# Attention scores from high and low halves of queries and keys in three single passes

## The chip, the cores and the metric

The kernel runs on one core of a Trainium2 chip. The metric is the device time of one execution, in microseconds. A core has TensorE for matrix products (PE, with its weight loads shown apart as PEld), VectorE (DVE), ScalarE (ACT), GpSimd (POOL) and SyncE (SP), which here only issues transfers. TensorE writes to PSUM, eight banks of 128 partitions by 512 float32.

## The reference

Two layers of cross attention are applied to `x` of shape (32, 256, 320). Each has 20 heads of 16 channels, and a context of 77 rows of 512 channels per batch. The context has exactly 77 rows, so only the text part of each layer has keys; the slices for objects, others and images are empty.

```python
q = split_heads(x @ Wq); k = split_heads(ctx @ Wk); v = split_heads(ctx @ Wv)
p = softmax(q @ k.T / sqrt(16))          # over the 77 keys
x = merge_heads(p @ v) @ Wo + bo + x     # layer 0, then layer 1 with its own weights
```

All of it is float32.

## The kernel before

Everything lies with channels on the partitions. Two batches make a pair, and one pair in one layer is a unit `u`; there are 32 units, taken in an order in which layer 0 runs four pairs ahead of layer 1. A unit's 320 channels by two batches are held as five groups `g` of 128 channels by 256 positions (`NG = 5`, `of_group`); the fifth group holds the last 64 channels of both batches. A group has eight heads. Four row blocks `j` of 32 channels hold two heads each, which the code counts by `e`.

Per unit, in the order of the data:

- `queries` or `outputs_and_queries` project the queries `q`; `keys` and `keys_rest` project the keys `kR` (two groups, two groups, one group). ACT copies them out of PSUM. `mask_keys` makes `kT`: for each `e` the keys with the other head's channels set to zero, on POOL (for unit 0 on DVE).
- `maxima` multiplies queries by `kT` for some halves `h` of a group (128 positions each, ten halves in a unit) into four banks `psm`, one for each `j`, and DVE reduces each bank to the largest score of every position and head. `turn` transposes those maxima on DVE into `mT` and writes them by small transfers into rows of the queries: one spare channel of the other head carries the maximum.
- `less_keys` makes `kM` on POOL: the masked keys with -1 in that spare channel, so that `scores` gets score less maximum from one product. As the spare channel belongs to the other head, the queries exist twice (`q[0]`, `q[1]`, the second a copy by a transfer).
- `scores(u, g)` makes the eight products of a group into four banks `pss`; ACT takes the exponential into `pT`. `products` multiplies by the values into one bank `po`, with a column of ones for the sums; `divide` transposes it on DVE (`turned`), takes the reciprocal (`inv`) and multiplies on POOL (`normal`); `turn_back` transposes on DVE into `oT`. `outputs_and_queries` projects the outputs of one unit (`psy`) and the queries of another. `vals` projects the values of a chunk of context rows (`psv`), and `place_vals` puts them in place by transfers.

All PSUM tiles come from one pool of eight banks handed out in turn (`bank`). The order of the instructions is written by hand: each step is put at a slot and a place in the slot (`at`), and each engine carries out its own instructions strictly in that order. `start(u)` is the first slot of unit `u`; four units take 17 slots. Within a slot the places follow one another in this order:

```python
    order = (
        "load", "maxima", "turn back", "turn", "scores", "values", "rest", "back", "full", "last",
    )
```

With `s = start(u - 2)`, a unit's keys stand at `s - 2`, `s - 1` and `s + 1` ("rest"; the last is `keys_rest`), its queries at `s`, its maxima from `s + 1` on, up to three halves a slot and none in a slot with two score groups, and its scores from `start(u)`. Units with `u % 4 > 0` have their first two score groups in one slot. The products of a group stand one slot after its scores.

Of the kernel before, what the change touches and what calls it, by code (L numbers as in the profile page):

```python
# [51 lines left out]

F32 = mybir.dt.float32
AF = mybir.ActivationFunctionType
ALU = mybir.AluOpType
AX = mybir.AxisListType
# [3 lines left out]
P = 128  # L60
# [34 lines left out]
def xattn_kernel(ctx: ExitStack, tc: tile.TileContext, xT, cT, cP, weights, outT):  # L95
# [14 lines left out]
    xs, cs, cvs = {}, {}, {}  # L110

    def load_x(p):
        x_sb = io.tile([P, NX], F32, tag="x", name=f"x_{p}", bufs=AHEAD + 3)
        xs[p] = x_sb
        if p == 0:
            for a, b in ((0, NT), (NT, 2 * NT), (2 * NT, NX)):
                nc.sync.dma_start(out=x_sb[:, a:b], in_=xT[p, :, a:b])
        else:
            (nc.scalar if p == 1 else nc.sync).dma_start(out=x_sb, in_=xT[p])
# [34 lines left out]
    make_identity(nc, ident)  # L154


    stages, maxes = [[], []], []
    for layer in range(2):
        for i in range(2):

            v = const.tile([P, HEADS // 2, 2, 2, HD], F32, name=f"stage_{layer}_{i}")
            nc.gpsimd.memset(v, 1.0)
            stages[layer].append(v)
    for i in range(2):
        m = const.tile([P, 2 * NG, 32], F32, name=f"max_{i}")
        nc.gpsimd.memset(m, 0.0)
        maxes.append(m)

    ctx.enter_context(tc.manual_schedule())

# [4 lines left out]
    nc.vector.tensor_reduce(masks, r32.rearrange("p (e d) -> p e d", d=HD), AX.X, ALU.add)  # L175

    less = const.tile([P, 2], F32, name="less")
    for e in range(2):
        i = HD * (1 - e)
        nc.vector.tensor_scalar_mul(less[:, e : e + 1], r32[:, i : i + 1], -1.0)  # L180


    warm = bank("warm")
# [80 lines left out]
        for e in range(2):  # L264
            engine.tensor_scalar_mul(kT[:, e], kR[:, groups], masks[:, e : e + 1])  # L265

    def less_keys(u):

        kR = st[u].pop("kr")
        kM = st[u]["km"] = work.tile([P, 2, NG, L], F32, tag="kM", name=f"kM_{u}", bufs=3)  # L270
        for e in range(2):
            nc.gpsimd.tensor_scalar(
                kM[:, e], kR, masks[:, e : e + 1], less[:, e : e + 1], ALU.mult, ALU.add
            )

    def keys(u, t):
        p, layer = units[u]
# [32 lines left out]
        mask_keys(u, 2)  # L310

    def new_queries(u):
        st[u]["q"] = [
            work.tile([P, NX], F32, tag=f"q{e}", name=f"q{e}_{u}", bufs=3) for e in range(2)
        ]
        return st[u]["q"][0]

    def queries(u):

        p, layer = units[u]  # L320
        w = w_sb[layer]
        q0 = new_queries(u)
        ps = [[bank(f"psq_{u}_{t}_{b}") for b in range(NB)] for t in range(2)]
        if u == 0:

            main_channels(ps, w["q"], xs[p], start=True, stop=False)
            last_channels(ps, w["q2"], xs[p], start=False, stop=True)
        else:
# [9 lines left out]
        if u > 0:  # L338
            nc.sync.dma_start(out=st[u]["q"][1], in_=q0)

    def queries_rest(u):

        p, layer = units[u]
        w = w_sb[layer]
        q0, q1 = st[u]["q"]
# [3 lines left out]
        nc.sync.dma_start(out=q1, in_=q0)  # L349

    def outputs_and_queries(u, uq):

        w, wq, o, x = w_sb[units[u][1]], w_sb[units[uq][1]], st[u]["o"], xs[units[uq][0]]
        q0 = new_queries(uq)
        y = [[bank(f"psy_{u}_{t}_{b}") for b in range(NB)] for t in range(2)]
        main_channels(y, w["o"], o, start=True, stop=False)
        y2 = bank(f"psy_{u}_2")
        rest_main(y2, w["o"], o, start=True, stop=False)


        q2 = bank(f"psq_{uq}_2")
# [24 lines left out]

    def load_chunk(layer, i):
        n = min(P, B * L - i * P)
# [41 lines left out]
    def place_vals(u, i):  # L430

        p, layer = units[u]
        if "v" not in st[u]:
            st[u]["v"] = work.tile(
                [P, NB, HEADS // 2, 2, 2, HD], F32, tag="v", name=f"v_{u}", bufs=3
            )
        for b in range(NB):
            first = (p * NB + b) * L
# [16 lines left out]
    def maxima(*parts):  # L455
# [1 line left out]
        ps = [bank(f"psm_{parts[0][0]}_{parts[0][1]}_{j}") for j in range(4)]  # L457
        steps = [(u, h) for u, first, n in parts for h in range(first, first + n)]
        for i, (u, h) in enumerate(steps):
            g, c = h // 2, h % 2  # L460
            q, kT = of_group(st[u]["q"][0], g), st[u]["k", g // 2]
            for j in range(4):
                r = slice(32 * j, 32 * j + 32)
                nc.tensor.matmul(  # L464
# [6 lines left out]
        for j in range(4):  # L471
            at = 0
            for u, first, n in parts:
                nc.vector.tensor_reduce(  # L474
                    maxes[u % 2][:, first : first + n, 2 * j : 2 * j + 2],
                    ps[j][:, at * 2 * L : (at + n) * 2 * L].rearrange(
                        "p (c e k) -> p c e k", e=2, k=L
                    ),
# [3 lines left out]
                at += n  # L482

    def turn(u):
        mT = work.tile([P, 2 * NG * 32], F32, tag="mT", name=f"mT_{u}", bufs=2)
        nc.vector.transpose(mT, maxes[u % 2].rearrange("p k i -> p (k i)"))
        for e in range(2):
            q = st[u]["q"][e].rearrange("(j i) n -> i j n", i=32)[HD * (1 - e)]
            for a in range(P // 32):
                queue = nc.scalar if u == 0 and a == 3 else nc.sync  # L490
                queue.dma_start(
                    out=q.rearrange("j (k a n) -> a j k n", a=P // 32, n=32)[a],
                    in_=mT[32 * a + e : 32 * a + 8 : 2].rearrange("j (k n) -> j k n", n=32),
                )


    def scores(u, g):
        kM = st[u]["km"]
        ps = [bank(f"pss_{u}_{g}_{j}") for j in range(4)]
        for e in range(2):  # L500
            q = of_group(st[u]["q"][e], g)
            for j in range(4):
                r = slice(32 * j, 32 * j + 32)
                nc.tensor.matmul(  # L504
                    ps[j][:L, e * S : (e + 1) * S], kM[r, e, g, :], q[r, :],
                    start=True, stop=True,
                )
        st[u]["p", g] = [probs.tile([P, 512], F32, tag="pT", name=f"pT_{u}_{g}_{j}") for j in range(4)]
        for j in range(4):
            nc.scalar.activation(st[u]["p", g][j][:L], ps[j][:L], AF.Exp, scale=SCALE)  # L510

    def products(u, g):
        vpad = st[u]["v"]
        if "o" not in st[u]:
            st[u]["o"] = work.tile([P, NX], F32, tag="oT", name=f"oT_{u}", bufs=3)
        po = bank(f"po_{u}_{g}")
        pT = st[u].pop(("p", g))
        for e in range(2):
# [106 lines left out]
    for u, (p, layer) in enumerate(units):  # L625
# [82 lines left out]
    at(-6, "rest", lambda: less_keys(0))  # L708
# [4 lines left out]
    at(-1, "rest", lambda: less_keys(1))  # L713
# [5 lines left out]
    for u, slot in ((1, 1), (2, 4)):  # L719
# [34 lines left out]
def pack(wq, wk, wv, wo, bias):  # L754

    out = np.zeros((P, WIDE), np.float32)

    def put(name, rows):
        at, n, width = PARTS[name]
# [72 lines left out]
```

## Time and profile before

| | |
|---|---|
| time, median of 3 runs | 949.21 us (948.82 to 950.74) |
| span of the profiled execution | 947.2 us |
| median of the runs less that span | 2.0 us |
| granted TensorE clock in the profiled execution | 1.000 |
| chain that ended last | PE 99% |
| its largest lines | po 16.6%, psy 15.3%, pss 15.1%, psq 14.8%, psm 11.3%, psv 8.8%, psk 7.2% |
| DMA, mean over the span | 88 GB/s, 83.78 MB |
| q copied to q by transfer | 32 issues of 640 KB |
| maxima into the queries | 254 issues of 5 KB on SP |

The page was taken on one execution; the profile gives no time for that execution other than its span, and the times are those of runs without a profile. A busy share is that of the whole span. A wait is put down to what ended last; the idle time before a group of instructions is that of the engine just before them. Matmuls are pipelined, so the busy time of a group is not the time that it takes from the others: that is read from the distance of starts.

### The profile page before, as it was taken

To read this page: it belongs to the slowest core of one execution; us is meant where nothing else is said; L and a number is where in the kernel's file an instruction comes from. 1 tells how busy PE (TensorE), PEld (TensorE's weight loads), DVE (VectorE), ACT (ScalarE), POOL (GpSimd) and SP (SyncE) were. 2 spreads that over 40 slices of the span, in tenths; PEclk is the share of its full clock that TensorE was granted. 3 is DMA by queue.
4 is the path that set the end of the run, shared out by engine and by line. 5 is a ranking of instruction groups with operands and counts; after the bars stand their busy time and mean duration, and the time that the engine had idled before them with its cause. 6 is when DMAs were issued, how large, how long until landed. Compare 5 with 4: busy or idle time off the path is not lost.

```text
span 947.2 us, 46546 instructions
## 1 busy us (share of the span) xinstructions
PE 940.9 (99%) x20942; PEld 630.3 (67%) x20942; DVE 533.2 (56%) x1195; ACT 431.8 (46%) x975; POOL 254.0 (27%) x422
## 2 busy tenths in 40 slices
PE   9999999999999999999999999999999999999998
PEld 7666766666666676667766666666667666666654
DVE  3465545655555555555656565655555655665564
ACT  2355343553435544355434455335454454544562
POOL 2233212332123321223322233212332223332211
PEclk9999999999999999999999999999999999999999
DMA  6553112232132321323222222322222221222102
GB/s 228 191 160 111 60 58 61 87 127 62 72 105 68 112 71 69 108 72 99 74 74 94 71 96 74 116 67 90 72 85 90 89 89 37 75 93 63 51 33 85
DMA packets 54825, 83.78 MB, mean 88 GB/s; under 512 B 15780, under 2 KB 36580, under 8 KB 54626
## 3 DMA queue, kind: packets, MB, share of 16 engines
q1 hardware_dynamic: 53674, 78.29, 25.4%
q8 instruction: 165, 2.70, 1.2%
q10 hardware_dynamic: 952, 2.50, 0.7%
q14 instruction: 34, 0.28, 0.1%
HBM read 35.39 MB, written 10.49 MB: 48 GB/s over the span
## 4 chain that ended last, share of the span: by engine, by line
PE 99%; DVE 0%; issue 0%
PE po L524 17%; PE psy L194 15%; PE pss L504 15%; PE psq L194 15%; PE psm L464 11%; PE psv L194 9%; PE psk L194 7%; PE psy L228 4%; PE psq L228 4%; PE psk L302 2%; PE warm L185 0%; PE psv L418 0%; DVE max L474 0%; DVE x L566 0%; DVE ones L152 0%
## 5 line engine op out<-in xcount | busy, mean ns | idle before, releaser
L510 ACT ACTIVATE pT<-pss 77x512 f32<-77x512 f32 x640 | 324.4, 593 | 191.3 <-PE pss L504 190.4
L474 DVE TENSOR_REDUCE max<-psm 128x6 f32<-128x462 f32 (+2 forms) x512 | 248.5, 550 | 242.7 <-PE psm L464 242.7
L545 POOL TENSOR_TENSOR normal<-turned,inv 128x256 f32<-128x256 f32 x160 | 99.1, 620 | 655.6 <-DVE inv L540 655.6
L524 PE MATMUL po<-pT,v 77*32 77x256 f32 x2560 | 165.9, 384 | 0.1
L194 PE MATMUL psy<-oT,w 128*32 128x256 f32 (+1 forms) x3072 | 164.4, 380 | 0.0
L504 PE MATMUL pss<-q,kM 32*77 32x256 f32 x2560 | 163.9, 376 | 0.0
L194 PE MATMUL psq<-x,w 128*32 128x256 f32 (+1 forms) x3072 | 151.5, 379 | 0.0
L194 PEld LDWEIGHTS psy<-oT,w 128*32 128x32 f32 (+1 forms) x3072 | 88.2, 108 | 63.6 <-issue 14.8
L536 DVE STREAM_TRANSPOSE turned<-po 128x512 f32<-128x512 f32 x160 | 109.2, 682 | 34.8 <-PE po L524 34.8
L524 PEld LDWEIGHTS po<-pT,v 77*32 77x32 f32 x2560 | 72.3, 109 | 80.2 <-DVE max L474 34.0
L194 PEld LDWEIGHTS psq<-x,w 128*32 128x32 f32 (+1 forms) x3072 | 86.1, 109 | 53.1 <-ACT pT L510 0.9
L265 POOL TENSOR_SCALAR kT<-kR,masks 128x154 f32<-128x154 f32 x186 | 111.7, 612 | 20.2 <-ACT kR L291 20.2
L504 PEld LDWEIGHTS pss<-q,kM 32*77 32x77 f32 x2560 | 98.8, 141 | 26.8 <-DVE oT L559 4.0
L464 PE MATMUL psm<-kT,q 32*128 32x154 f32 x2560 | 115.4, 306 | 0.0
L464 PEld LDWEIGHTS psm<-kT,q 32*128 32x128 f32 x2560 | 89.7, 183 | 32.7 <-issue 24.8
L566 DVE SCALAR_TENSOR_TENSOR x<-psy,w,x 128x256 f32<-128x256 f32 x160 | 69.2, 478 | 73.2 <-PE psy L194 72.0
L194 PE MATMUL psv<-w,cv 128*32 128x160 f32 x2432 | 93.6, 299 | 0.3 <-DVE max L474 0.3
L559 DVE STREAM_TRANSPOSE oT<-normal 128x256 f32<-128x256 f32 x160 | 67.4, 433 | 43.1 <-POOL normal L545 43.1
L381 ACT COPY q<-psq 128x256 f32<-128x256 f32 x28 | 10.4, 372 | 162.0 <-PE psq L228 162.0
L194 PEld LDWEIGHTS psv<-w,cv 128*32 128x32 f32 x2432 | 77.9, 110 | 4.3 <-DVE max L474 0.7
L194 PE MATMUL psk<-c,w 128*32 128x154 f32 x2048 | 78.8, 294 | 0.0
L194 PEld LDWEIGHTS psk<-c,w 128*32 128x32 f32 x2048 | 66.2, 110 | 11.9 <-DVE max L474 0.6
(35 smaller groups left out, 449.0 us busy)
## 6 DMA issues: line engine op xcount, KB each, us to landing
q<-q SPq DMA_DIRECT2D x32, 640.0 KB
c<-in_cP_dram SPq DMA_DIRECT2D x32, 308.0 KB
cv<-in_cT_dram SPq DMA_DIRECT2D x38, 256.0 KB
out_dram<-x SPq DMA_DIRECT2D x15, 640.0 KB
x<-in_xT_dram SPq DMA_DIRECT2D x14, 640.0 KB
v<-stage SPq DMA_DIRECT2D x26, 192.5 KB
q<-mT SPq DMA_DIRECT2D x254, 5.0 KB
w<-in_w_dram ACTq DMA_DIRECT2D x2, 640.0 KB
```

The source lines that it names most:

```text
L194: nc.tensor.matmul(out[m : m + 32], lhsT[:, m : m + 32], rhs, **flags)
L228: nc.tensor.matmul(ps[o : o + 32, 0:S], lhsT, rhs, **flags)
L265: engine.tensor_scalar_mul(kT[:, e], kR[:, groups], masks[:, e : e + 1])
L464: nc.tensor.matmul(ps[j][:, i * 2 * L : (i + 1) * 2 * L], q[r, c * P : (c + 1) * P], kT[r, :, g % 2, :], start=True, stop=True,)
L474: nc.vector.tensor_reduce(maxes[u % 2][:, first : first + n, 2 * j : 2 * j + 2], ps[j][:, at * 2 * L : (at + n) * 2 * L].rearrange("p (c e ...
L504: nc.tensor.matmul(ps[j][:L, e * S : (e + 1) * S], kM[r, e, g, :], q[r, :], start=True, stop=True,)
L510: nc.scalar.activation(st[u]["p", g][j][:L], ps[j][:L], AF.Exp, scale=SCALE)
L524: nc.tensor.matmul(po[o : o + 32, e * S : (e + 1) * S], vpad[:L, b, pair, e].rearrange("p a d -> p (a d)"), pT[j][:L, e * S : (e + 1) * S] ...
L536: nc.vector.transpose(turned[:, 0 : 2 * S], po)
L545: nc.gpsimd.tensor_tensor(normal.rearrange("p q e d -> p e q d"), outs, inv.unsqueeze(3).broadcast_to([P, 2, S // 32, HD]), ALU.mult,)
L559: nc.vector.transpose(of_group(st[u]["o"], g), normal)
L566: nc.vector.scalar_tensor_tensor(x, ps[:, 0:S], w_sb[layer]["b"][:, 0, t : t + 1], x, ALU.add, ALU.add)
```

## The change

The kernel no longer puts the maximum in a spare channel and no longer multiplies in float32 for the scores. Queries and keys are split into a high half, rounded by writing it as `float32r`, and a low half, the exact rest. The score product then has 16 channels times two query halves on its 32 rows; the keys stand there twice, and one matmul with the keys' high half and one with their low half add up. Ahead of them, one matmul of 512 columns with a constant of -1 (`less`) and the split maxima as rows (`max_rows`) writes the maximum into each bank. All are `float32r`. The maxima themselves stay float32 products.

The halves are made by POOL (for unit 0 by DVE), `split_keys` and `split_queries` in three pieces, and put in place by SP's transfers, `spread_keys` (four a unit) and `spread_queries` (twelve a unit). `turn` splits the maxima on DVE before the transpose and issues four transfers. The heads of a pair are interleaved by channel (`pack` reorders the columns of the weights on the host), so the masks change. In `maxima` the half `h` now is group `h % 5`, position block `h // 5`. `v`, `oT` and the new tiles have two buffers, `x` six instead of seven; the values are made one unit later.

```diff
     def load_x(p):
-        x_sb = io.tile([P, NX], F32, tag="x", name=f"x_{p}", bufs=AHEAD + 3)
+        x_sb = io.tile([P, NX], F32, tag="x", name=f"x_{p}", bufs=AHEAD + 2)
...
+    maxes = const.tile([P, 2, 4, 32], F32, name="maxes")
...
+        m = const.tile([P, 2, 512], F32R, name=f"max_rows_{i}")
...
+    k_halves = const.tile([P, NG, 2, L], F32R, name="k_halves")
...
+    less = const.tile([P, 4, L], F32R, name="less")
+    nc.gpsimd.tensor_scalar_mul(less, rows.unsqueeze(2).broadcast_to([P, 4, L]), -1.0)
...
-    def less_keys(u):
-
-        kR = st[u].pop("kr")
-        kM = st[u]["km"] = work.tile([P, 2, NG, L], F32, tag="kM", name=f"kM_{u}", bufs=3)
+    def split(engine, high, low, x):
+
+        engine.tensor_copy(high, x)
+        engine.tensor_tensor(low, x, high.bitcast(F32), ALU.subtract)
+
+    def split_keys(u):
+
+        split(nc.gpsimd if u else nc.vector, k_halves[:, :, 0], k_halves[:, :, 1], st[u].pop("kr"))
+
+    def spread_keys(u):
+
+        kS = st[u]["ks"] = work.tile([P, 2, NG, 2, L], F32R, tag="kS", name=f"kS_{u}", bufs=2)
         for e in range(2):
-            nc.gpsimd.tensor_scalar(
-                kM[:, e], kR, masks[:, e : e + 1], less[:, e : e + 1], ALU.mult, ALU.add
-            )
+            for r in range(2):
+                nc.sync.dma_start(
+                    out=kS.bitcast(F32).rearrange("(d r) e g h k -> r e d (g h k)", r=2)[r, e],
+                    in_=k_halves.bitcast(F32).rearrange("(d e) g h k -> e d (g h k)", e=2)[e],
+                )
+
+    PIECES = ((0, NT), (NT, 2 * NT), (2 * NT, NX))
+
+    def split_queries(u, i):
+
+        a, b = PIECES[i]
+        x = st[u]["halves", i] = work.tile(
+            [P, 2, NT], F32R, tag="halves", name=f"halves_{u}_{i}", bufs=2
+        )
+        split(
+            nc.gpsimd if u else nc.vector, x[:, 0, : b - a], x[:, 1, : b - a], st[u]["q"][:, a:b]
+        )
+
+    def spread_queries(u, i):
+
+        a, b = PIECES[i]
+        if i == 0:
+            st[u]["qs"] = work.tile([P, 2, NX], F32R, tag="qs", name=f"qs_{u}", bufs=2)
+        to = st[u]["qs"].bitcast(F32).rearrange("(d h) e n -> h e d n", h=2)
+        x = st[u].pop(("halves", i)).bitcast(F32).rearrange("(d e) h n -> e h d n", e=2)
+        for e in range(2):
+            for h in range(2):
+                nc.sync.dma_start(out=to[h, e, :, a:b], in_=x[e, h, :, : b - a])
...
-        nc.sync.dma_start(out=st[uq]["q"][1], in_=q0)
...
-            g, c = h // 2, h % 2
-            q, kT = of_group(st[u]["q"][0], g), st[u]["k", g // 2]
+            g, c = h % NG, h // NG
+            q, kT = of_group(st[u]["q"], g), st[u]["k", g // 2]
...
     def turn(u):
-        mT = work.tile([P, 2 * NG * 32], F32, tag="mT", name=f"mT_{u}", bufs=2)
-        nc.vector.transpose(mT, maxes[u % 2].rearrange("p k i -> p (k i)"))
+
+        m = st[u].pop("m").rearrange("p e (c g) j -> p (e c) g j", g=NG)
+        to = maxes.rearrange("p t y (j g i) -> p t i y g j", j=4, i=2)
+        for t in range(2):
+            n = 4 - 3 * t
+            new = m[:, :, 4 * t : 4 * t + n]
+            high, low = (to[:, t, i, :, 0:n] for i in range(2))
+            nc.vector.tensor_copy(high.bitcast(F32R), new)
+            nc.vector.tensor_tensor(low, new, high, ALU.subtract)
+        mT = work.tile([P, 2 * 4 * 32], F32, tag="mT", name=f"mT_{u}", bufs=1)
+        nc.vector.transpose(mT, maxes.rearrange("p t y i -> p (t y i)"))
+        for a in range(4):
+            nc.sync.dma_start(
+                out=max_rows[u % 2].bitcast(F32).rearrange(
+                    "(r x) t (y a n) -> x a r (t y) n", x=4, a=4, n=32
+                )[0, a],
+                in_=mT[32 * a : 32 * a + 32].rearrange("r (y n) -> r y n", n=32),
+            )
+
+
+    def scores(u, g):
+        ps = [bank(f"pss_{u}_{g}_{j}") for j in range(4)]
+        for j in range(4):
+            r = slice(32 * j, 32 * j + 32)
+            nc.tensor.matmul(
+                ps[j][:L], less[r, g % 4, :], max_rows[u % 2][r, g // 4], start=True, stop=False
+            )
         for e in range(2):
...
-    def scores(u, g):
-        kM = st[u]["km"]
-        ps = [bank(f"pss_{u}_{g}_{j}") for j in range(4)]
-        for e in range(2):
-            q = of_group(st[u]["q"][e], g)
-            for j in range(4):
-                r = slice(32 * j, 32 * j + 32)
-                nc.tensor.matmul(
-                    ps[j][:L, e * S : (e + 1) * S], kM[r, e, g, :], q[r, :],
-                    start=True, stop=True,
-                )
+            q = of_group(st[u]["qs"][:, e], g)
+            for half in range(2):
+                for j in range(4):
+                    r = slice(32 * j, 32 * j + 32)
+                    nc.tensor.matmul(
+                        ps[j][:L, e * S : (e + 1) * S], st[u]["ks"][r, e, g, half, :], q[r, :],
+                        start=False, stop=(half == 1 and e == 1),
+                    )
...
         if u > 1:
-            at(s + 2, "rest", lambda u=u: less_keys(u))
+            at(s + 2, "split", lambda u=u: split_keys(u))
+            at(start(u - 1), "load", lambda u=u: spread_keys(u))
+            for i in range(3):
+                at(start(u - 1) + i - 1, "split", lambda u=u, i=i: split_queries(u, i))
+                at(start(u - 1) + i, "load", lambda u=u, i=i: spread_queries(u, i))
...
-        first = (-6, -2)[u] if u < 2 else s + 1
+        first = (-6, -2)[u] if u < 2 else start(u - 1) + 1
...
-        "load", "maxima", "turn back", "turn", "scores", "values", "rest", "back", "full", "last",
+        "load", "maxima", "turn back", "turn", "scores", "values", "rest", "back", "split", "full", "last",
```

More of the change, by code (lines that the diff above doesn't have):

```diff
@@ L53 @@
 F32 = mybir.dt.float32
+F32R = mybir.dt.float32r
 AF = mybir.ActivationFunctionType
@@ L154, in xattn_kernel @@
     make_identity(nc, ident)
-    stages, maxes = [[], []], []
+    stages = [[], []]
     for layer in range(2):
@@ L163, in xattn_kernel @@
             stages[layer].append(v)
+    maxes = const.tile([P, 2, 4, 32], F32, name="maxes")
+    nc.gpsimd.memset(maxes, 0.0)
+    max_rows = []
     for i in range(2):
-        m = const.tile([P, 2 * NG, 32], F32, name=f"max_{i}")
-        nc.gpsimd.memset(m, 0.0)
-        maxes.append(m)
+        m = const.tile([P, 2, 512], F32R, name=f"max_rows_{i}")
+        nc.gpsimd.memset(m.bitcast(F32), 0.0)
+        max_rows.append(m)
+    k_halves = const.tile([P, NG, 2, L], F32R, name="k_halves")
     ctx.enter_context(tc.manual_schedule())
@@ L174, in xattn_kernel @@
     masks = const.tile([P, 2], F32, name="masks")
-    nc.vector.tensor_reduce(masks, r32.rearrange("p (e d) -> p e d", d=HD), AX.X, ALU.add)
-    less = const.tile([P, 2], F32, name="less")
-    for e in range(2):
-        i = HD * (1 - e)
-        nc.vector.tensor_scalar_mul(less[:, e : e + 1], r32[:, i : i + 1], -1.0)
+    nc.vector.tensor_reduce(masks, r32.rearrange("p (d e) -> p e d", e=2), AX.X, ALU.add)
+    rows = const.tile([P, 4], F32, name="rows")
+    nc.vector.tensor_reduce(
+        rows, r32.rearrange("p (g i x) -> p g i x", i=2, x=4)[:, :, :, 0], AX.X, ALU.add
+    )
+    less = const.tile([P, 4, L], F32R, name="less")
+    nc.gpsimd.tensor_scalar_mul(less, rows.unsqueeze(2).broadcast_to([P, 4, L]), -1.0)
     warm = bank("warm")
@@ L312, in new_queries @@
     def new_queries(u):
[L313 to L316, printed above, removed]
+        st[u]["q"] = work.tile([P, NX], F32, tag="q", name=f"q_{u}", bufs=3)
+        return st[u]["q"]
     def queries(u):
@@ L337, in queries @@
             nc.scalar.copy(of_group(q0, g), ps[g // 2][g % 2][:, 0:S])
-        if u > 0:
-            nc.sync.dma_start(out=st[u]["q"][1], in_=q0)
     def queries_rest(u):
@@ L344, in queries_rest @@
         w = w_sb[layer]
-        q0, q1 = st[u]["q"]
+        q0 = st[u]["q"]
         ps = bank(f"psq_{u}_2")
@@ L348, in queries_rest @@
         nc.scalar.copy(of_group(q0, 4), ps[:, 0:S])
-        nc.sync.dma_start(out=q1, in_=q0)
     def outputs_and_queries(u, uq):
@@ L434, in place_vals @@
             st[u]["v"] = work.tile(
-                [P, NB, HEADS // 2, 2, 2, HD], F32, tag="v", name=f"v_{u}", bufs=3
+                [P, NB, HEADS // 2, 2, 2, HD], F32, tag="v", name=f"v_{u}", bufs=2
             )
@@ L473, in maxima @@
             for u, first, n in parts:
+                if "m" not in st[u]:
+                    st[u]["m"] = work.tile([P, 2, 2 * NG, 4], F32, tag="m", name=f"m_{u}", bufs=2)
                 nc.vector.tensor_reduce(
-                    maxes[u % 2][:, first : first + n, 2 * j : 2 * j + 2],
+                    st[u]["m"].rearrange("p e h j -> p h e j")[:, first : first + n, :, j],
                     ps[j][:, at * 2 * L : (at + n) * 2 * L].rearrange(
@@ L484, in turn @@
     def turn(u):
-        mT = work.tile([P, 2 * NG * 32], F32, tag="mT", name=f"mT_{u}", bufs=2)
-        nc.vector.transpose(mT, maxes[u % 2].rearrange("p k i -> p (k i)"))
-        for e in range(2):
[L488 to L493, printed above, removed]
-                )
@@ L497, in scores @@
-    def scores(u, g):
-        kM = st[u]["km"]
-        ps = [bank(f"pss_{u}_{g}_{j}") for j in range(4)]
-        for e in range(2):
-            q = of_group(st[u]["q"][e], g)
-            for j in range(4):
-                r = slice(32 * j, 32 * j + 32)
-                nc.tensor.matmul(
-                    ps[j][:L, e * S : (e + 1) * S], kM[r, e, g, :], q[r, :],
-                    start=True, stop=True,
-                )
+        m = st[u].pop("m").rearrange("p e (c g) j -> p (e c) g j", g=NG)
@@ new lines, in turn @@
+        for a in range(4):
[12 more added lines that the diff above has]
+            )
+        for e in range(2):
+            q = of_group(st[u]["qs"][:, e], g)
[5 more added lines that the diff above has]
+                        start=False, stop=(half == 1 and e == 1),
+                    )
@@ L514, in products @@
         if "o" not in st[u]:
-            st[u]["o"] = work.tile([P, NX], F32, tag="oT", name=f"oT_{u}", bufs=3)
+            st[u]["o"] = work.tile([P, NX], F32, tag="oT", name=f"oT_{u}", bufs=2)
         po = bank(f"po_{u}_{g}")
@@ L707, in xattn_kernel @@
     at(-7, "rest", lambda: queries_rest(0))
-    at(-6, "rest", lambda: less_keys(0))
+    at(-7, "split", lambda: split_keys(0))
+    at(-6, "load", lambda: spread_keys(0))
+    for i in range(3):
+        at(-6 + i, "split", lambda i=i: split_queries(0, i))
+        at(-5 + i, "load", lambda i=i: spread_queries(0, i))
     for slot, h, n in ((-6, 0, 3), (-6, 3, 3), (-4, 6, 2), (-4, 8, 2)):
@@ L712, in xattn_kernel @@
     at(-4, "last", lambda: queries(1))
-    at(-1, "rest", lambda: less_keys(1))
+    at(-3, "split", lambda: split_keys(1))
+    at(-2, "load", lambda: spread_keys(1))
+    for i in range(3):
+        at(-3 + i, "split", lambda i=i: split_queries(1, i))
+        at(-2 + i, "load", lambda i=i: spread_queries(1, i))
     for slot, h, n in ((-2, 0, 3), (-2, 3, 2), (0, 5, 3)):
@@ L756, in pack @@
     out = np.zeros((P, WIDE), np.float32)
+    turned = np.arange(C).reshape(-1, 2, HD).transpose(0, 2, 1).reshape(-1)
+    wq, wk = np.asarray(wq)[:, turned], np.asarray(wk)[:, turned]
     def put(name, rows):
@@ L813 @@
     arrays = {f"in_{k}_dram": np.ascontiguousarray(v) for k, v in arrays.items()}
-    nc = bacc.Bacc("TRN2", target_bir_lowering=False, num_devices=1)
+    nc = bacc.Bacc("TRN2", target_bir_lowering=False, num_devices=1, dynamic_dma_scratch_size=4096)
     t = {
```

## The prediction

> **What bounds the kernel now.** The page's first part comes first: PE is busy all the time and no other engine more than 56%.
>
> ```profile
> PE 940.9 (99%) x20942; PEld 630.3 (67%) x20942; DVE 533.2 (56%) x1195; ACT 431.8 (46%) x975; POOL 254.0 (27%) x422
> ```
>
> So the end is PE's sum, and an edit counts through what it does to PE's rows or to a wait in PE's queue. The groups by line and the chain give the size of the edited part:
>
> ```profile
> L504 PE MATMUL pss<-q,kM 32*77 32x256 f32 x2560 | 163.9, 376 | 0.0
> L504 PEld LDWEIGHTS pss<-q,kM 32*77 32x77 f32 x2560 | 98.8, 141 | 26.8 <-DVE oT L559 4.0 <-issue 2.1 <-DVE turned L536 0.4
> 64.19 3.46 PE psy L194 x64
> ```
>
> The program has 160 groups of 8 score products, 1280; the trace has 2560, so a float32 product runs as two matmuls. Four run side by side (four row groups of the array): 64 matmuls of 256 columns in 3.46 us is 54 ns each, 216 ns for a set of four. A score group is four sets, 0.86 us.
>
> Third, the longest waits in front of PE's weight loads, since a tight queue shows there what stands just behind PE:
>
> ```profile
> PEld po L524 <- DVE max L474: 34.0, 91, 0.4
> PEld po L524 <- ACT pT L510: 9.7, 26, 0.4
> ```
>
> The products after the scores are released last by the maxima's reduction 91 times, by the exponentials 26 times. Last, the timeline of one slot (start, duration, engine, line, count), a two-half slot, and a slot with two score groups:
>
> ```profile
> 312.91 0.25 DVE L540 RECIPROCAL inv<-turned 128x16 f32<-128x16 f32 x1
> 313.60 1.20 POOL L545 TENSOR_TENSOR normal<-turned,inv 128x256 f32<-128x256 f32 x2 [13.87 <-DVE inv L540]
> 314.23 1.07 PE L464 MATMUL psm<-kT,q 32*128 32x154 f32 x24
> 314.77 0.94 POOL L265 TENSOR_SCALAR kT<-kR,masks 128x77 f32<-128x77 f32 x2
> 315.13 1.04 PE L504 MATMUL pss<-q,kM 32*77 32x256 f32 x16
> 315.32 2.28 DVE L474 TENSOR_REDUCE max<-psm 128x6 f32<-128x462 f32 x4 [1.31 <-PE psm L464]
> 316.10 1.07 PE L524 MATMUL po<-pT,v 77*32 77x256 f32 x16
> ...
> 291.87 1.04 PE L504 MATMUL pss<-q,kM 32*77 32x256 f32 x16
> 292.06 1.63 DVE L474 TENSOR_REDUCE max<-psm 128x4 f32<-128x308 f32 x4 [0.73 <-PE psm L464]
> 292.84 1.07 PE L524 MATMUL po<-pT,v 77*32 77x256 f32 x16
> ...
> 323.16 1.97 PE L504 MATMUL pss<-q,kM 32*77 32x256 f32 x32
> 324.34 3.98 ACT L510 ACTIVATE pT<-pss 77x512 f32<-77x512 f32 x8 [0.76 <-PE pss L504]
> 325.06 1.07 PE L524 MATMUL po<-pT,v 77*32 77x256 f32 x16
> ```
>
> **The scores themselves.** From 315.13 to 316.10 is 0.97 us: 0.86 for the sets and 0.11 for the turn to another tiling (the same 0.11 stands between most kinds of product). The new group has one set of 512 columns and four of 256, each one matmul instead of two. No one-pass product is in the trace. A set of 256 columns lies between half of a float32 set (108 ns: two matmuls, each with twice the columns' time) and a whole one (216 ns). I take 108, assuming that each of a float32 product's two equal matmuls sweeps its columns twice where a rounded operand needs one sweep; the trace cannot test that, so the upper end is a rival below. 216 + 4 x 108 = 0.65 us, 0.21 less. The Trainium skill, FP8 and Floating Point Precision, TensorE Precision Notes, counts four passes for true float32 and describes a reduced read of it, which would put a set at the lower end too; no row here shows it.
>
> Can the weights follow that fast? The maxima take (315.13 - 314.23 - 0.11) / 6 = 0.13 us a set with weights of 128 columns (a load of 183 ns each), so loads of 77 columns (141 ns) limit a set to no more than 0.13. The Trainium skill, TensorE: Matmul & The Clock Gate, Packing small matmuls, says that a weight load overlaps running matmuls only when its row group differs, which speaks against the change: the next set uses the same four row groups, so a set would be 141 + 108 ns and the group, with 141 + 216 for its first set, 1.35 us, 0.49 longer than now. The maxima's 0.13 us under loads of 183 ns contradicts it, and the row decides.
>
> **Where the 0.21 us goes.** PSUM's eight banks are handed out in turn: four to the maxima, four to the scores, and po gets the first maxima bank back, once DVE has reduced it. That reduction starts at 315.32, when the maxima end, lasts 0.64 (tile view), and po starts 0.14 later, at 316.10. Shorter scores do not move it: in these 91 slots the gain is nothing, and PE waits instead. In the 16 slots with two halves the reduction lasts 0.48: 292.06 + 0.48 + 0.14 = 292.68, so 0.16 of 0.21 is kept: 2.6 us. In 22 slots with two groups po waits for ACT's first exponential (324.34 + 0.59 + 0.13 = 325.06), which starts when the first group is complete: one group's 0.21 is kept, not two: 4.6 us. Five groups have neither: 1.0 us. Together -8.2 us where 160 x 0.21 = 33.6 was taken out.
>
> **The new order of the maxima.** The half h was group h // 2; now it is group h % 5. Group 4's masked keys (kT of 77 columns) are made last: keys_rest stands in slot s + 1, and POOL masks them after the slot's normal products, which wait for DVE. Group 4 was halves 8 and 9, slots later; now it is half 4, in the very next slot. In the rows above, POOL ends them at 315.71; half 4 as second of three starts at 314.23 + 0.37 = 314.60. With 0.05 us from POOL's end to the reader (normal to oT), PE waits 1.15 us, with the scores, po and everything later queued behind. I worked out the same difference for every unit (u mod 4 sets which place half 4 gets):
> - u mod 4 = 1: half 4 comes a slot later, spare 2.9 us or more. Nothing.
> - u mod 4 = 2 or 3, fifteen units: 1.15 us in ten; 0.06 in the five (6, 14, 23, 26, 31) where the slot before holds 64 value products instead of 32, as the change moves them by a unit: 11.8 us.
> - u mod 4 = 0, seven units: third place, yet 1.45 us by the rows, since another unit's turn and a mixed reduction delay DVE. turn grows by two copies and two subtractions of 64 and 16 elements: between 144 ns (the one-element TENSOR_SCALAR) and 254 ns (RECIPROCAL of 16) each, 0.6 to 1.0, less 0.05 for a transpose of 256 columns (433 ns) instead of 320 (484): 0.75. That is 2.2 in five, 1.1 in unit 16 (64 value products) and 2.6 in unit 28 (the short value chunk): 14.7 us.
> - u = 2: half 4 is first of slot 3, 53.38, and the keys end at 55.12: 1.8 us.
> Sum 28.3 us. After each of these 23 waits the weights' load is bare again, 0.11: 2.5 us.
>
> **The rest.** POOL loses kM (two of 0.65 us a unit) and gets a copy and a subtraction over 385 and 1280 elements. Nearest rows: kM 385 in 661 ns, normal 256 in 620, kT 154 in 612: 1.7 to 4 ns an element, 5.7 to 13 us a unit; I take 2.2, 7.3 us, nearest to kM and normal. POOL goes from 8 to about 14 of 29.6 us a unit. The cover is thin in one place: the first query piece, 2.3 us, runs just before the last group's normal and pushes it from 327.37 to 328.2 (it starts behind that slot's masks at 325.91); oT follows 1.1 later, and PE needs it at 330.37, 1.0 us after that. At 4 ns an element the piece ends at 330.0, the cover is gone, and PE waits about 0.7 us x 24. The DMAs: 20 a unit on SP instead of 9, 0.54 us each, 10.8 us of 29.6 beside some 6 for the loads, stores and value rows; those queued behind them are asked for two slots ahead. kS, qs and the maximum rows are read three or more slots after issue. I cost them at nothing. Two small terms: at the start DVE splits unit 0's queries between two batches of reductions whose banks PE wants at 21.95: +1.0 us (0 to 2). Where turn stands before two score groups (u mod 4 = 1, seven times), turned frees po's bank 0.75 later while the scores ask for it 0.2 earlier; the old spare leaves 0.35: +2.4 us (0 to 4). Buffers cut to two (v, oT, qs, kS) and x to six are free a slot or more ahead.
>
> **Sum.** -8.2 + 28.3 + 2.5 + 1.0 + 2.4 = +26 us on the profiled span of 947.2: 973. The median of the runs shown, 949.21, is 2.0 above the span, so 975 us.
>
> **Rivals.**
> - Masks in time (faster). If POOL has group 4 ready when PE comes, 30.8 us fall away: 949.2 - 8.2 + 3.4 = 944. It decides where the waits sum to under 5 us, that is kT about 1.1 us earlier in each such slot. For it: POOL was idle 13.87 us before its normals. Against: the masks stand behind two normals in POOL's order, and those behind DVE. 0.08.
> - po not held. If the 91 slots keep their 0.21, 19 us less: 956. For it: PE shows hardly more than 0.11 idle there now. Against: po starts 0.14 us after the reduction in slot after slot, and the slots with two reductions have 0.19. 0.08.
> - POOL too slow: 4 ns an element or more, normal late, DVE's oT and PE's outputs behind it: 15 us or more on top, 990 and up. 0.15.
> - One pass is no cheaper than one of the two matmuls now: 6 x 0.216 (the long set counts twice), 1.30 us a group, +0.44 x 160 = 70 us, and nothing of the 8.2 gained: 1053. For it: every row of 256 columns has 216 ns. Against: a product's second matmul takes as long as its first, so the pair does more than one rounded product, and the whole of it costs four times 108. 0.05.
> The forecast has 0.62; 0.02 is left for a time within 0.2%, about the least a measurement of this kernel can tell from no change.
>
> **How the numbers follow.** The low end, 956, is po not held; the high end, 996, takes in turn at its upper price, both small terms at theirs and the lighter part of POOL's case. Outside lie masks in time (0.08), the one-pass case (0.05) and the heavy part of POOL's (0.06). Faster 0.08, same 0.02, slower 0.90.
>
> **What would show it.** Right: psm with about 25 to 30 us of waits on POOL kT in PE's weight loads, a score group about 0.65 us long, and po still 0.14 us after the first reduction, its wait on DVE up from 34 us by some 19. Wrong: no wait on kT; a score group near 0.86 or above; PE waiting for a DMA (qs, kS, maximum rows) or for oT behind POOL.

## The result, and the profile after

The changed kernel takes 1076.45 us (1069.82 to 1078.75, 4 runs), the kernel before 949.09 us on the same chip: a ratio of 1.1328, 95% interval 1.1292 to 1.1364. The forecast was slower, but with 975 us and a range that ended at 996. The profiled execution has a span of 1077.0 us against 947.2, so 129.8 us are to be explained.

The page of the changed kernel, busy time first and then the row of the granted clock (40 slices, tenths of full speed):

```profile
PE 969.4 (90%) x21582; PEld 659.8 (61%) x21582; DVE 567.8 (53%) x1330; ACT 432.9 (40%) x975; POOL 407.9 (38%) x608
...
PEclk9969999899998999989999898998999989899899
```

PE is no longer busy all the time, and its mean clock is 0.944 where it was 1.000. No other engine is near its limit: POOL went from 254 to 408 us and is still idle most of the time. So the new time is waits, and something that lowers the clock. The waits in front of PE's matmuls (total, times, longest):

```profile
PE pss L546 <- DMA max_rows<-mT: 61.3, 9, 8.1
PE psm L499 <- POOL kT L273: 30.4, 21, 2.5
PE psy L202 <- DVE oT L609: 6.4, 7, 1.2
```

The second line is the wait that the prediction worked out, at the size that it gave (30.8). The first is one that it had costed at nothing, and the largest. Eight of its nine stand about 132 us apart, one for every four units, at u mod 4 = 0. This is the timeline of the third, maxima and turn of unit 10 and the score products of unit 8:

```profile
334.25 0.81 PE L499 MATMUL psm<-kT,q 32*128 32x154 f32 x16
335.07 1.64 DVE L511 TENSOR_REDUCE m<-psm 128x4 f32<-128x308 f32 x4 [0.62 <-PE psm L499]
336.98 0.18 DVE L529 CAST maxes<-m 128x64 fp32r<-128x64 f32 x1
...
337.82 0.45 DVE L532 STREAM_TRANSPOSE mT<-maxes 128x256 f32<-128x256 f32 x1
338.33 2.68 SPq L534 DMA_DIRECT2D max_rows<-mT  x4
342.65 0.71 PE L546 MATMUL pss<-max_rows,less 32*77 32x512 f32 x4 [7.60 <-DMA max_rows<-mT]
```

Follow the slots in the code: `slot_of(8, 4)` is 38, and the last halves of unit 10 are in slot 38 too, so `turn(10)` stands there, at the place "turn", ahead of "scores". Both use `max_rows[u % 2]`, and 8 and 10 are both even. So `turn(10)` overwrites the rows before `scores(8, 4)` reads them, and the first products of that group wait for the whole chain of another unit: reductions, turn, four transfers from one queue, landing. (Group 4 of unit 8 then has unit 10's maxima subtracted. A shift common to all 77 keys drops out of the softmax; the wait does not.) The maximum rows of unit 10 itself are first read in slot 43.

The windows view of the same stretch (length; busy time of PE, PEld, DVE, ACT, POOL; granted clock; DMA share; GB/s) shows a second cost behind the first:

```profile
334.00:338.00 4.00, 1.05 (x28) 0.58 (x17) 3.24 (x12) 0.68 (x2) 1.95 (x3) 1.00 0.16 47
338.70:342.60 3.90, 0.00 (x0) 0.00 (x0) 0.00 (x0) 0.00 (x0) 0.00 (x0) 0.50 0.24 36
342.60:349.00 6.40, 6.35 (x84) 4.00 (x88) 1.41 (x3) 2.33 (x5) 1.03 (x2) 0.51 0.33 126
349.00:352.70 3.70, 3.66 (x80) 2.32 (x76) 0.97 (x2) 3.24 (x7) 3.11 (x5) 1.00 0.11 40
```

PE's work before the wait ends at 335.06. At 338.7 the granted clock falls to a half, and it stays there for 10.24 us, 6.3 of them after PE has work again. The records show fifteen such stretches ahead of the end, of 3.41, 6.83 or 10.24 us, eight behind the long waits for the maximum rows and seven behind waits of 1.9 to 2.5 us for `kT`: 119.5 us in all. PE works in 83 us of them, at half speed (a row of 32 `psk` matmuls takes 2.28 us there and 1.24 elsewhere), which costs about 41.5 us.

The accounts, on the span: 61.3 (maximum rows) + 30.4 (`kT`) + 6.4 (`oT`) + 41.5 (clock) - 14.2 (what the shorter scores gave, below) = 125.4 of 129.8 us. The 14.2 is an estimate. The 4.4 us left were not traced.

### The profile page after: what moved, and what is told of

Read it like the earlier page. It is cut to its first block, busy times and chain, and to the rows that moved or that the text cites. A ratio compares the mean times of both kernels' runs of the same rounds, so it can differ in the third digit from the quotient of the medians.

```text
span 1077.0 us, 48805 instructions
## 1 busy us (share of the span) xinstructions
PE 969.4 (90%) x21582; PEld 659.8 (61%) x21582; DVE 567.8 (53%) x1330; ACT 432.9 (40%) x975; POOL 407.9 (38%) x608
## 4 chain that ended last, share of the span: by engine, by line
PE 63%; DVE 11%; issue 10%; POOL 9%; DMA 4%; SPq 2%; POOLq 0%; ACT 0%
PE psy L202 11%; PE psq L202 11%; PE po L574 10%; PE psm L499 7%; DVE m L511 6%; PE psk L202 6%; PE pss L554 6%; POOL kT L273 4%; PE psv L202 4%; PE pss L546 3%; PE psy L236 3%; PE psq L236 3%; POOL halves L278 2%; SPq L534 2%; DMA max_rows<-mT 2%
## 5 line engine op out<-in xcount | busy, mean ns | idle before, releaser
L511 DVE TENSOR_REDUCE m<-psm 128x6 f32<-128x462 f32 (+2 forms) x512 | 248.4, 551 | 270.2 <-PE psm L499 269.7
L574 PE MATMUL po<-pT,v 77*32 77x256 f32 x2560 | 179.0, 408 | 3.3
L499 PE MATMUL psm<-kT,q 32*128 32x154 f32 x2560 | 124.6, 315 | 30.4 <-POOL kT L273 30.4
L546 PE MATMUL pss<-max_rows,less 32*77 32x512 f32 x640 | 83.6, 495 | 61.5 <-DMA max_rows<-mT 61.3
L499 PEld LDWEIGHTS psm<-kT,q 32*128 32x128 f32 x2560 | 92.8, 186 | 68.9 <-POOL kT L273 36.0
L554 PE MATMUL pss<-qs,kS 32*77 32x256 f32 x2560 | 111.6, 289 | 0.0
L278 POOL TENSOR_TENSOR halves<-q,halves 128x512 fp32r<-128x512 f32 (+1 forms) x93 | 102.4, 1101 | 7.8
L554 PEld LDWEIGHTS pss<-qs,kS 32*77 32x77 f32 x2560 | 96.0, 151 | 12.7 <-issue 1.3
L202 PE MATMUL psk<-c,w 128*32 128x154 f32 x2048 | 90.7, 324 | 0.5 <-DVE m L511 0.5
L202 PEld LDWEIGHTS psk<-c,w 128*32 128x32 f32 x2048 | 72.7, 123 | 20.3 <-issue 5.2
```

The lines of the kernel that those rows point to most:

```text
L202: nc.tensor.matmul(out[m : m + 32], lhsT[:, m : m + 32], rhs, **flags)
L278: engine.tensor_tensor(low, x, high.bitcast(F32), ALU.subtract)
L499: nc.tensor.matmul(ps[j][:, i * 2 * L : (i + 1) * 2 * L], q[r, c * P : (c + 1) * P], kT[r, :, g % 2, :], start=True, stop=True,)
L511: nc.vector.tensor_reduce(st[u]["m"].rearrange("p e h j -> p h e j")[:, first : first + n, :, j], ps[j][:, at * 2 * L : (at + n) * 2 * L]. ...
L546: nc.tensor.matmul(ps[j][:L], less[r, g % 4, :], max_rows[u % 2][r, g // 4], start=True, stop=False)
L554: nc.tensor.matmul(ps[j][:L, e * S : (e + 1) * S], st[u]["ks"][r, e, g, half, :], q[r, :], start=False, stop=(half == 1 and e == 1),)
```

## The experiments

Ratios are to the kernel before, in runs on the same chip.

**Turn behind the scores** (`e1_turn_after_scores`). Only the order in a slot changes, so that `scores(8, 4)` reads unit 8's own rows and the transfers of `turn(10)` come after.

```diff
-        "load", "maxima", "turn back", "turn", "scores", "values", "rest", "back", "split", "full", "last",
+        "load", "maxima", "turn back", "scores", "turn", "values", "rest", "back", "split", "full", "last",
```

> The change with one edit: within a slot, turn is placed after scores instead of before it, so that the fifth score group of a unit with u mod 4 = 0 no longer reads maximum rows that turn of unit u + 2 rewrites in the same slot. Theory: the 62 us that PE waits for max_rows<-mT (8 times 7.8) come from that order alone, and the half clock behind each of these waits (8 windows of 10.2 us, about 3.1 us lost in each) goes with them: 1076 - 62 - 25 = 989 us; the wait for kT stays at about 32 us. Rival: the transfers themselves are late, behind twelve query transfers a unit on SP; then a wait for max_rows, qs or kS of similar size stays and the time is above 1040 us.

Measured: 992.84 us, ratio 1.0455 (1.0440 to 1.0471). PE's waits:

```profile
PE psm L499 <- POOL kT L273: 31.2, 21, 2.9
PE psy L202 <- DVE oT L609: 6.3, 7, 1.2
PE pss L546 <- DMA max_rows<-mT: 1.6, 1, 1.6
```

Moving one word is worth 84 us, more than the 61.3 us of the wait itself: the half clock behind it goes too (from 119.5 us to 23.9). The rival is out: with the same transfers on SP only 1.6 us of waits for the rows are left.

**Group 4's halves last** (`e2_group4_last`). The maxima take groups 0 to 3 first and group 4 as halves 8 and 9, as before the change. A reduction that crosses half 8 is cut in two; the rest is the changed kernel.

```diff
-            g, c = h % NG, h // NG
+            g, c = (h % 4, h // 4) if h < 8 else (4, h - 8)
...
+                if first < 8:
+                    cut.append((u, first, min(n, 8 - first)))
+                if first + n > 8:
+                    cut.append((u, max(first, 8), first + n - max(first, 8)))
+            for u, first, n in cut:
...
-            new = m[:, :, 4 * t : 4 * t + n]
+            new = m[:, 64 * t : 64 * t + 16 * n].rearrange("p (a g j) -> p a g j", a=4, j=4)
```

> The change with the maxima's halves in another order: groups 0 to 3 for both position blocks first, group 4 in halves 8 and 9 as in the kernel before (m is laid out so that turn still reads it; a reduction that crosses half 8 is cut in two). Theory: the waits of psm for POOL's kT (32 us over 21 waits) are gone, and the short half-clock windows behind them (41 us of clock loss in all, less 25 behind the other waits, so 16): 1076 - 48 = 1028 us. Rival: POOL is late because of the added splits, not because of the order; then psm still waits for kT and the time is above 1060 us.

Measured: 1032.36 us, ratio 1.0879 (1.0856 to 1.0902). PE's waits:

```profile
PE pss L555 <- DMA max_rows<-mT: 62.9, 9, 8.4
...
PE psm L499 <- POOL kT L273: 3.7, 2, 2.0
```

The waits for `kT` fall from 30.4 to 3.7 us, two at the start; those for the maximum rows stay at 62.9. The new order of the maxima costs 44 us, of which 27 are the wait and 16 the clock (41.5 down to 25.7 us by the same working).

**Work in the wait** (`warm_in_wait`). To tell the clock from the wait, the changed kernel gets 32 products of ones with ones, into a bank that the scores then overwrite, ahead of each `scores(u, 4)` with u mod 4 = 0.

```diff
+        if g == 4 and u % 4 == 0:
+            for _ in range(32):
+                nc.tensor.matmul(ps[0][:, 0:P], ones, ones, start=True, stop=True)
```

> The change with 32 idle float32 products of ones (128 x 128, about 6.9 us) written to the first score bank ahead of the fifth score group of units with u mod 4 = 0, where PE otherwise stands 7.8 us; the bank is overwritten by the scores. Theory: the low clock (10.2 us windows at 0.5) follows PE's idleness, so the wait stays as it is, the clock stays at 1.0 there, and 8 times 3.1 us come back: 1076 - 25 = 1051 us. Rival: the clock is lowered by the new single-pass products themselves or by something else; then the windows stay and the time is 1076 us or more.

Measured: 1053.25 us, ratio 1.1104 (1.1075 to 1.1133): 23 us less than the changed kernel with more work and with the same rows waited for. What PE still waits for those rows, and the row of the clock on its page:

```profile
PE pss L549 <- DMA max_rows<-mT: 3.9, 8, 1.0
...
PEclk9979999999999999999999999999999999999999
```

The half clock fell from 119.5 to 23.9 us, none of it behind the eight long waits. So it follows PE's idleness, and not the new form of the products, which this kernel has as well. The Trainium skill, TensorE: Matmul & The Clock Gate, Part 1, puts the clock at half after an idle window of 3.4 us that runs free. The window agrees with the rows: the half-clock stretches of a run last one to four times 3.41 us and start a whole number of 3.41 us apart. That PE must idle for a whole one does not: waits of 2.1 us halve the clock too, and one of 1.1 (last section).

**Both undone** (`e3_both`). Turn behind the scores and group 4's halves last.

> Both edits: turn after scores and group 4 last. If the two waits and the half clock that follows them are the whole loss, 1076 - 87 - 48 = 941 us, below the kernel before by some 8 us, with a clock of 1.0 throughout; what is left is the wait of psy for oT (7.5 us, seven times) in the slots where turn delays DVE. Rival: when these waits are gone others take their place (SP's 20 transfers a unit, POOL at 14 of 30 us): above 955 us.

Measured: 956.95 us, ratio 1.0078 (1.0063 to 1.0093). The changed kernel took 127.4 us more than the one before, and 7.0 are left of it. Yet 941 was expected, and the rival's "above 955 us" is met: other waits take the place, though behind `turn` on DVE and not behind SP. Two waits for `kT` are left at the start, 3.9 us with 5.1 us of clock behind them. In the middle of the kernel the `turn` of units with u mod 4 = 1 makes `oT` late (0.7 us for PE, seven times), and that of units with u mod 4 = 2 makes `turned` late in the next slot, one with two score groups (0.36 us more up to po than without the delay). The timeline of unit 9's (u mod 4 = 1):

```profile
276.23 1.28 POOL L278 TENSOR_TENSOR halves<-q,halves 128x512 fp32r<-128x512 f32 x1
276.34 0.43 DVE L618 STREAM_TRANSPOSE oT<-normal 128x256 f32<-128x256 f32 x1
276.69 0.90 DVE L538 CAST maxes<-m 128x64 fp32r<-128x64 f32 x1
277.63 0.28 DVE L539 TENSOR_TENSOR maxes<-m,maxes 128x64 f32<-128x64 f32 x1
...
280.32 0.45 DVE L618 STREAM_TRANSPOSE oT<-normal 128x256 f32<-128x256 f32 x1 [0.73 <-POOL normal L604]
...
280.82 0.42 PE L202 MATMUL psy<-oT,w 64*32 64x256 f32 x4 [0.69 <-DVE oT L618]
```

The copy of 64 elements takes 0.90 us, where it took 0.18 in the rows above. It ends at 277.59, 0.08 us after POOL's subtraction (276.23 + 1.28 = 277.51), and so in all seven such slots.

**Turn at the end of the slot** (`e4_turn_at_end`). The same kernel, with turn behind `back`.

```diff
-        "load", "maxima", "turn back", "scores", "turn", "values", "rest", "back", "split", "full", "last",
+        "load", "maxima", "turn back", "scores", "values", "rest", "back", "turn", "split", "full", "last",
```

> Both undone (turn behind the scores, group 4's halves last), and turn moved on behind the slot's other DVE work, to just before the splits. In e3_both 6.6 us of waits for oT and 0.36 us in each of 15 slots with two score groups (5.4 us) stood behind turn on DVE. Theory (turn, longer by its copies and subtractions and held up by POOL, delays turn back and turned, and nothing needs its result in that slot): 956.95 - 6.6 - 5.4 = 945, waits for oT under 1 us. Rival (it is the queries' split on POOL that delays normal and so oT; turn only stands beside it): 957 as before, with the waits for oT still there. Second rival: turn so late that the maximum rows are late for the scores again: 960 or more, with waits for max_rows.

Measured: 950.17 us, ratio 1.0009 (1.0001 to 1.0018). The waits for `oT` and the late second groups are gone, as the theory had it, but eleven new waits of po, ten of 0.45 us and one of 0.89, take 5.4 us back: where a slot of maxima follows, turn now stands ahead of its reductions. So the first rival is out: the queries' split on POOL is where it was.

**The start** (`e6_start_too`). The queries of unit 1 are split three slots later and unit 2's later keys (`keys` of its second groups, and `keys_rest`) made a slot earlier.

```diff
-            k = (0, 1, 2) if u == 2 else (s - 2, s - 1, s + 1)
+            k = (0, 0, 1) if u == 2 else (s - 2, s - 1, s + 1)
...
-        at(-3 + i, "split", lambda i=i: split_queries(1, i))
-        at(-2 + i, "load", lambda i=i: spread_queries(1, i))
+        at(i, "split", lambda i=i: split_queries(1, i))
+        at(1 + i, "load", lambda i=i: spread_queries(1, i))
```

> e4_turn_at_end, and at the start the queries of unit 1 are split three slots later and unit 2's last keys are made one slot earlier. In e3_both two waits for kT stood at 45.4 and 53.1 us, 4.2 us in sum, with 5.1 us lost at half clock behind them. Theory (POOL's first splits wait for the queries with unit 2's masks queued behind them, and the clock halves behind the wait): 945 - 9.3 = 936, no wait for kT over 0.3 us, and no half clock after the first 30 us. Rival (the splits moved later now make unit 1's scores wait for their transfers): the kT waits gone but a wait for qs of 2 to 4 us in their place, 941 to 945.

Measured: 947.18 us, ratio 0.9978 (0.9969 to 0.9986). The waits for `kT` are gone. The gain is 3.0 us of 9.3: a wait of po of 1.2 us, from 51.7 us on, with 3.4 us at half clock behind it, took part of their place. The waits of po for the reductions, the eleven and this one:

```profile
PE po L583 <- DVE m L520: 6.6, 12, 1.2
```

**Scores ahead of the maxima** (`e8_scores_first`). This tests whether po is held by the reduction.

```diff
-        "load", "maxima", "turn back", "scores", "values", "rest", "back", "turn", "split", "full", "last",
+        "load", "turn back", "scores", "maxima", "values", "rest", "back", "turn", "split", "full", "last",
```

> e6_start_too with the scores ahead of the maxima in each slot, so that po takes back a bank of the scores (freed by an exponential) and no longer one of the maxima (freed by DVE's reduction). Theory (the shorter scores gave 0.08 us in 75 slots with three halves where 0.17 was taken out, since po waits for the reduction that starts when the maxima end): 75 x 0.09 = 7 us less than e6, 929. Rival one (the 0.09 is not a hold but what one tiling's turn to another costs): no change, 936. Rival two (with the reductions a group later on DVE, turned, turn back and the next slot's banks are late): slower than e6, 940 or more, with weights of po or pss waiting for max.

Measured: 959.83 us, ratio 1.0116 (1.0103 to 1.0129). The theory is right about the hold, and the second rival about the time. In a typical three-half slot, maxima and scores together take 1.667 us up to po, against 1.786 in the kernel without this step and 1.866 before the change: without the hold, 0.20 us of the change's gain shows, close to the 0.21 that the prediction took out. But the weight loads of po now wait for the exponentials:

```profile
PEld po L583 <- ACT pT L569: 23.8, 120, 0.5
```

The two-half slots lose 0.23 us each, 14 of the slots with two groups 0.4 (their weight loads wait for a late `turned`), and 13 three-half slots 0.5, for a reason that was not traced. That eats more than the hold had cost. The rival had named waits for the maxima's reductions; in front of the weight loads of pss these are 2.6 us in three places.

**A piece of the queries earlier** (`e9_piece_earlier`). From the kernel with both undone; meant to take POOL's subtraction away from turn's copy.

```diff
-                at(start(u - 1) + i - 1, "split", lambda u=u, i=i: split_queries(u, i))
+                first_piece = u % 4 == 2 and u > 2 and i == 0
+                at(start(u - 1) + i - 1 - first_piece, "split", lambda u=u, i=i: split_queries(u, i))
```

> e3_both, where the first piece of the queries of units with u mod 4 = 2 is split on POOL one slot earlier, so that POOL's subtraction of 512 columns no longer runs beside turn's first copy on DVE. Theory (a copy of 64 elements on DVE, 0.18 to 0.27 us elsewhere, does not end before POOL's subtraction does, and so took 0.9 to 1.16 us in those slots): the copy takes 0.3 us or less in those units, the waits for oT fall from 6.6 us to about 1, time 951. Rival (the copy is slow for its own reasons, its strided output or the maxima it reads): still 0.9 us and more, time 957 as e3_both.

Measured: 962.61 us, ratio 1.0147 (1.0132 to 1.0161): a miss. The edit moved a piece that did not stand beside the copy, which keeps its 0.9 us, and put one beside another unit's turn. That shows the hold better than the edit meant would have:

```profile
299.34 1.29 POOL L278 TENSOR_TENSOR halves<-q,halves 128x512 fp32r<-128x512 f32 x1
299.42 1.36 DVE L539 TENSOR_TENSOR maxes<-m,maxes 128x64 f32<-128x64 f32 x1
...
302.22 0.46 PE L555 MATMUL pss<-max_rows,less 32*77 32x512 f32 x2 [1.10 <-DVE turned L595]
```

A subtraction that takes 0.28 us elsewhere takes 1.36 beside POOL's, in seven slots of seven, and ends 0.15 us after it. The 1.08 us go straight through `turned` to PE.

**Turn by unit** (`e10_turn_by_unit`). The kernel of the start's experiment, with turn behind the scores or at the slot's end by what DVE owes PE next.

```diff
+                at(slot, "turn" if u > 2 and u % 4 in (1, 2) else "turn early", lambda u=u: turn(u))
...
+        "load", "maxima", "turn back", "scores", "turn early", "values", "rest", "back", "turn", "split", "full", "last",
```

> e6_start_too, with turn behind the scores for units whose u mod 4 is 0 or 3 (and the first three), and at the slot's end only where u mod 4 is 1 or 2. In e6 11 waits of po of some 0.45 us stood behind turn, all in the slots of u mod 4 = 3 or 0, where a slot of maxima follows and turn stands ahead of its reductions (and one of 1.3 us at 51 us, unit 1); in e3_both, with turn behind the scores, those two kinds of slot lost no more than 0.08 us each, and the losses lay at u mod 4 = 1 (0.93 us, oT) and 2 (0.36 us, turned). Theory (each place of turn delays whatever DVE owes PE next, and that differs by unit): 947.2 - 11 x 0.37 - 1 = 942. Rival (the 0.45 us come from the hold between DVE and POOL, which falls on whatever stands at that time): 946 to 948.

Measured: 943.98 us, ratio 0.9937 (0.9924 to 0.9950). The eleven waits of po are gone; what is left of po's waits is

```profile
PE po L583 <- PE pss L563: 2.6, 16, 0.2
```

All longer waits of PE stand in the first 70 us. So the halves in single passes do beat the float32 scores, by 0.6%, once the steps around them are put in place. That the kernel before would gain nothing by such a reordering was not tested.

## Why the prediction was wrong

The sign was right, and the step that was meant to carry it was right too; the time lies 80 us above the top of the range because one step failed and one cost was not in the sum.

**The step that failed: "kS, qs and the maximum rows are read three or more slots after issue. I cost them at nothing."** It holds for `kS`, for `qs`, and for the maximum rows of the unit that was just turned (slot 38 to 43). It does not for the buffer: two buffers by `u % 2` mean that `turn(u)` also touches what unit u - 2 still has to read, and for u mod 4 = 2 `scores(u - 2, 4)` stands later in that very slot. The prediction asked when the new data are needed, and not who still needs the old. It did ask that of `v`, `oT`, `qs`, `kS` and `x`, "free a slot or more ahead", and left out `max_rows`. PE waiting for the maximum rows stands among its signs of being wrong, but with no price and no chance. The cost was 61 us of waits, and with their clock 84 us. With this one step undone the kernel takes 992.84 us, inside the forecast range.

**The cost not in the sum: the clock.** The prediction added waits at their own length. Of the changed kernel's excess about 41.5 us is work at half speed behind waits: 22.0 in the eight stretches behind the maximum rows and 19.6 in the seven behind `kT`. (With one kind of wait taken out the rest does not stay as it was: 25.7 are left without the waits for `kT`, 11.1 without those for the rows.) In the kernel before no wait of PE is longer than 1.0 us, and its clock is 1.000.

**Maxima's new order: right.** Waits for `kT` of 30.4 us in 21 places against 28.3 + 2.5 in 23. The 1.15 us "in ten" and 1.1 in unit 16 are 1.01 in twelve places, the 2.2 "in five" are 2.10 in five, the 2.6 of unit 28 are 2.52. The five waits of 0.06 are not there, and the start has 5.2 us in three places where 1.8 was forecast; that the sums agree so closely is partly luck. As a price it was still too low, because of the clock: undoing it alone gave 44 us.

**The scores: nearly right in what a group takes, wrong in where it goes.** Starts of 256-column sets lie 0.12 us apart (0.108 taken), so neither rival came true, neither a single pass at the price of one of the two matmuls nor weight loads that do not overlap. The set of 512 columns takes 0.34 us up to the next set where 0.216 was taken, but the scores now start 0.10 us earlier behind the maxima. Where nothing holds po the gain is 0.16 us (16 two-half slots, 1.602 to 1.444) to 0.20 (in the experiment with the scores first), with 0.21 expected. "In these 91 slots the gain is nothing" was the other mis-sized term. Of the 75 whose banks have one reduction each, 44 gain 0.08 in the changed kernel, and most of the others stand behind a wait; the 15 with two reductions for a bank gain 0.043. Now po starts 0.05 us after the reduction's recorded end. So the 0.14 of before was the 0.11 of the turn to another tiling, which happened to end just behind the reduction: PE was not yet held. The wait of po's weight loads for the reduction, forecast to rise from 34 us by some 19, fell:

```profile
PEld po L574 <- DVE m L511: 20.0, 81, 0.3
```

Taken for all 75, the sum is 75 x 0.08 + 16 x 0.158 + 22 x 0.229 + 15 x 0.043 = 14.2 us in place of 8.2. Counted slot by slot in the last kernel it is about 12: there 46 of the 75 gain 0.08, and 15, whose reduction that kernel cuts in two, lose 0.08.

**POOL: right in its rate, wrong in who meets it.** The first piece takes 0.61 + 1.28 = 1.9 us where 2.3 was taken, and normal still waits for `inv`, not for the pieces. But the "thin cover" broke from another side: turn's copy on DVE is held by POOL's subtraction, so `oT` is late by about 0.9 us in seven slots (6.4 us), which was outside the sum.

Of the rivals, "masks in time" describes what moving group 4 back does; its 944 needed the maximum rows out of the way as well, and the last kernel here, which has both, takes 944 us, though with other steps moved too. As far as the runs show, that agreement is chance.

## What to carry to other kernels

When a change gives a tile its buffers by turns, write down for each writer the last reader of the old contents and its place in the written order, not only the first reader of the new. A wait of TensorE, here mostly from some 2 us on, is to be priced with the work at half clock behind it, which came to a third of the long waits for the maximum rows and to two thirds of the waits for `kT`. And a long two-input step on GpSimd should be placed by what stands beside it on VectorE, not by whether GpSimd has time.

## What was not expected of the hardware

- In the changed kernel's eight waits of 7.5 us and more the granted clock halves 1.8 to 4.5 us after PE's work ends and stays so for 6.83 or 10.24 us. Behind seven of its eight waits of 1.9 to 2.5 us it halves for 3.41 to 10.24 us, mostly when PE is already at work again (PE back at 133.33, half clock from 133.9); behind its twelve of 1.0 us it does not. The length alone does not decide: in "A piece of the queries earlier" one wait of 1.1 us halves the clock (half from 888.9) and one of 3.3 us does not (at 51.0). Of the sixteen waits of 2.1 us in all runs eleven halve it, 1.85 to 3.8 us after PE's work ends. In the other five none of the points 3.41 us apart at which such stretches start lies between 1.7 and 4.3 us after it. Thirty-two small products in a long wait keep the clock up.
- DVE's copies and subtractions from SBUF do not end while a subtraction or product of two tiles runs on POOL: 0.18 us becomes 0.90 to 1.16, 0.28 becomes 1.36, and 0.72 beside `normal` (with turn at the slot's end). In the rows above DVE's transpose of 256 columns at 276.34, which starts beside the same subtraction, keeps its 0.43. The subtraction of 16 elements takes 0.19 us inside a mask on POOL (a product of one tile), in nearly all places, as it does alone. The Trainium skill, Trainium Architecture — The Big Picture, What this means for kernel authors, calls the port that DVE and GpSimd share an exclusive lock and not a split of the bandwidth. The ends 0.08 to 0.15 us after POOL's agree with that; the transpose and the mask show that not every pair of instructions meets there.
